# The last band of both 3x3 convolutions in mixed form, inside an attention-and-convolution kernel on one Trainium2 core

## The chip, the cores and the metric

The kernel runs on one core of a Trainium2 chip. The metric is the device time of one execution in microseconds (us); of several executions the median is taken. The engines are named as in the profile: PE is TensorE (PEld its weight loads), DVE is VectorE, ACT is ScalarE, POOL is GpSimd, SP is SyncE, which here only issues DMAs.

## The reference, cut to what matters

The input `x` is (4, 128, 64, 64) in float32: four images, 128 channels, 64 x 64 positions. Layer 0 is a group norm, a 4-head attention over the 4096 positions of each image, a projection and a residual. Layer 1, where the change lies, is a block of two 3x3 convolutions with weights quantized to 3 bits; its own input is the residual:

```python
residual = x
out = conv3x3_decomposed(x, lsq_quantize(w1, alpha1))
out = jax.nn.relu(batchnorm(out, gamma1, beta1))
out = conv3x3_decomposed(out, lsq_quantize(w2, alpha2))
out = batchnorm(out, gamma2, beta2)
out = jax.nn.relu(out + residual)
```

`batchnorm` takes the mean and the variance of each channel over all four images, so nothing behind a convolution can start before its last output is counted.

## The kernel before, in words

**Two parts.** Some nine tenths of the time go to the attention, in which the change touches nothing. Behind it come the two convolutions, one call each of `layer(i, prepare)`, with i = 0 and 1, and then a last pass that scales, adds the residual, applies relu and writes the output. All instructions stand in the order in which the code issues them; each engine runs its own in that order.

**Bands.** A convolution goes through 16 bands, four for each image. A band is 16 output rows, 1024 outputs for each channel, two PSUM banks of 512. `bandlist` holds them, and band m is its m-th entry, counted from 0; the last is band 15. Both operands of the convolution are float32 split in a high and a low part, so each product is done twice.

**Plain form.** `conv` (L830) computes 512 outputs with 18 matmuls of 512 columns, nine taps for the high and nine for the low part: 36 for a band. Its input is prepared by one cast on ACT (L619) and one subtraction on DVE (L622). It lies in rows of 66 columns with an empty column at each side (`raw_band`, L562), so in convolution 0 its load lands in runs of 64 elements; that of a band in mixed form has no side columns and lands in one run for each channel.

**Mixed form.** Two neighbouring output rows share work: from sums and differences of input rows and of weights (`mix_weights`) four products are formed, each three taps by two parts, six matmuls of 512 columns: 24 for a band (`conv_by_two`, L863). Two of them are the inner products a[0] and a[1], of which the even rows need the sum and the odd rows the difference; c[0] and c[1] are the outer products, one for the even and one for the odd rows. The price lies on the other engines. The input is prepared by `mixed_parts`: three subtractions and sums on DVE (`vo` L600, `vi` L602 and L603), two casts on ACT (`uo` and `ui`, L605), two more subtractions on DVE (`lo` and `li`, L609) and four small memsets on POOL (L596). The output is put together by `rows_of_two`: ACT copies a[1] (L886), DVE forms both inner results into the output `cv` (L889, L891), and the outer products are added either by a copy on ACT (L896 for one tile of two banks, L902 for two tiles of one) and an accumulating DMA that POOL issues (L904), or at once on DVE (L908). `BY_TWO` names the bands in mixed form: 2 to 14 before, of both convolutions.

**PSUM.** `banks(m)` hands out the banks of a mixed band. The inner products get a tile of two banks of the pool `pss` (three such tiles); the outer products get, in turn, either another `pss` tile (the names end in z) or two one-bank tiles of the pool `psa` (x and y; the pool has two).

**Order within a band.** The PE work of band m comes first, then `prepare(m)` gives the input preparation of band m + 2 (`begin`, `rest`) and the fetch of band m + 3 (`later`): in convolution 0 a load by SP (L628), in convolution 1 a relu on ACT that reads `cv` (L1147). On DVE the order is: the first three steps for band m + 2, the inner results of band m, the two last steps for band m + 2, and, where they are added at once, the outer results of band m. In convolution 0, bands 13 and 14 are added at once, and so in convolution 1 (`m > 12`).

**Statistics.** Plain bands go through `bn_stats` on DVE. For mixed bands the sums come with the instructions that form the outputs, and the sum of squares from a pass of ACT over the band (L1020), which can only run once the accumulating DMA has landed. These passes stand in the list `behind`, and `flush(1)` issues all but the newest.

**The end of a convolution.** `flush()` issues the squares that are left; DVE folds statistics into `end` (L1036 to L1044); the last band is done in plain form, half after half, with `bn_stats` (L1050) and a copy by ACT (L1051) for each; PE does ten small matmuls to stay busy (`keep_warm`, L315); `batch_norm` forms scale and shift (L926 to L935). In convolution 0 the next one then starts with relu on ACT (L1159).

**Residual loads.** The last pass needs the attention's output again (`load_res`, L1184). SP issues eight of these loads (512 KB each) as soon as the load of band 15 in convolution 0 is out, and eight more late in convolution 1, when the buffers of the pools `upper` and `kpool` come free.

Of the kernel before, what the change touches and what calls it, by code (L numbers as in the profile page):

```python
# [16 lines left out]
F32 = mybir.dt.float32  # L17
AF = mybir.ActivationFunctionType
ALU = mybir.AluOpType
# [3 lines left out]
P = 128  # L23
# [55 lines left out]
def _fast_body(ctx, tc, x, norm_w, norm_b, qkv_wt, qkv_b, proj_wt, proj_b,  # L79
# [152 lines left out]
    def f32(t):  # L232
        return t.bitcast(F32)
# [347 lines left out]

    BY_TWO = (set(range(2, 15)),) * 2

    def mixed_parts(t, name):

# [275 lines left out]
    def conv_by_two(parts, a, c, i):  # L863

        for m, ps, w in ((1, a[0], wmix[:, 0, :, :]), (2, a[1], wmix[:, 1, :, :]),
                         (0, c[0], wq[i][:, 0:3, :]), (3, c[1], wmix[:, 2, :, :])):
            n = 0
            for part in parts:
                for kw in range(3):
                    nc.tensor.matmul(ps.rearrange("p (r w) -> p r w", w=W), w[:, kw, :],  # L870
                                     part[m][:, :, kw : kw + W], start=(n == 0), stop=(n == 5))
                    n += 1

    def rows_of_two(a, c, both, y, sums, name, at_once):

        def of(t, e):
            return t.rearrange("p (r e w) -> p r e w", e=2, w=W)[:, :, e, :]

        even, odd = of(y, 0), of(y, 1)
        a0, a1, c0, c1 = (u.rearrange("p (r w) -> p r w", w=W) for u in (*a, *c))  # L880
        outer_rows = f32(stack_tile(f"co{name}"))[:, : 2 * FB]

        copied = outer_rows[:, :FB].rearrange("p (r w) -> p r w", w=W)

        def copy():
            nc.scalar.copy(copied, a1)  # L886

        def inner():
            nc.vector.scalar_tensor_tensor(even, copied, 1.0, a0, ALU.mult, ALU.add,  # L889
                                           accum_out=sums[:, 0:1])  # L890
            nc.vector.scalar_tensor_tensor(odd, copied, -1.0, a0, ALU.mult, ALU.add,  # L891
                                           accum_out=sums[:, 1:2])

        def outer():
            if both is not None:
                nc.scalar.activation(  # L896
                    outer_rows.rearrange("p (r e w) -> p e r w", e=2, w=W),
                    both.rearrange("p e (r w) -> p e r w", w=W), AF.Identity,
                    accum_out=sums[:, 2:3])
            else:  # L900
                for e, u in enumerate((c0, c1)):
                    nc.scalar.activation(of(outer_rows, e), u, AF.Identity,  # L902
                                         accum_out=sums[:, 2 + e : 3 + e])
            nc.gpsimd.dma_start(out=y, in_=outer_rows, accum_op=ALU.add)  # L904

        def outer_at_once():
            for e, u, v in ((0, even, c0), (1, odd, c1)):
                nc.vector.scalar_tensor_tensor(u, u, 1.0, v, ALU.mult, ALU.add,  # L908
                                               accum_out=sums[:, e : e + 1])

        return copy, inner, outer_at_once if at_once else outer, outer_rows
# [26 lines left out]
    def layer(i, prepare, start=None):  # L938
# [6 lines left out]
        sums = mid.tile([P, 4 * len(two)], F32, name=f"sums{i}")  # L945
        squares = mid.tile([P, len(two)], F32, name=f"squares{i}")
        shift = mid.tile([P, 2], F32, name=f"shift{i}")
        end = mid.tile([P, 18], F32, name=f"end{i}")
        n_plain, n_two = (float(len(u) * 2 * FB) for u in (plain, two))
        nc.gpsimd.memset(end[:, 0:1], n_plain)  # L950
        nc.gpsimd.memset(sums, 0.0)
# [4 lines left out]
        def flush(left=0):  # L956
            while len(behind) > left:
                behind.pop(0)()
# [26 lines left out]
        def banks(m):  # L985
            b, g = bandlist[m]
            a = conv_tile(i, b, g)
            if (len(two) - 1 - two.index(m)) % 2:
                c = [psa.tile([P, FB], F32, name=f"c{i}_{b}_{g}{j}", tag="a") for j in "xy"]
                both = None  # L990
            else:
                both = pss.tile([P, 2, FB], F32, name=f"c{i}_{b}_{g}z", tag="s")
                c = [both[:, j, :] for j in range(2)]
            return [a[:, j, :] for j in range(2)], c, both

        done = start(banks, stats, keep, origin) if start else {}
        for m, (b, g) in enumerate(bandlist[:-1]):
            if m in done and m not in BY_TWO[i]:
                continue
            begin, rest, later = prepare(m)  # L1000
            if m in BY_TWO[i]:
                if m in done:
                    a, c, both = done[m]
                else:
                    a, c, both = banks(m)
                    conv_by_two(ready[i, b, g], a, c, i)
                y = cv[b][:, 2 * g * FB : (2 * g + 2) * FB]
                k = two.index(m)
                copy, inner, outer, junk = rows_of_two(a, c, both, y, sums[:, 4 * k : 4 * k + 4], f"{i}_{m}",
                                                       m > 12)  # L1010
                copy()
                if i == 0 and m < 13:
                    flush(1)
                begin()
                flush(1)
                inner()
                rest()
                later()
                outer()
                behind.append(lambda y=y, k=k, junk=junk: nc.scalar.activation(  # L1020
                    junk, y, AF.Square, bias=shift[:, 1:2], accum_out=squares[:, k : k + 1]))
                continue
            ps = conv_tile(i, b, g)
            for j in range(2):
                conv(ready[i, b, g], ps[:, j, :], j, wq[i])
            begin()
            flush(1)
            rest()
            later()
            for j in range(2):  # L1030
                stats(m, j, ps)
                keep(m, j, ps)
            if m == 0:
                origin()
        flush()
        nc.vector.bn_aggr(end[:, 1:3], st.rearrange("p j s -> p (j s)"))  # L1036
        nc.vector.tensor_scalar(end[:, 2:3], end[:, 2:3], n_plain, None, ALU.mult)
        nc.vector.tensor_reduce(end[:, 4:5], sums, AX.X, ALU.add)
        nc.vector.tensor_reduce(end[:, 5:6], squares, AX.X, ALU.add)
        nc.vector.tensor_scalar(end[:, 4:5], end[:, 4:5], 1.0 / n_two, None, ALU.mult)  # L1040
        off = small.tile([P, 1], F32, name=f"off{i}", tag="rs")
        nc.vector.tensor_tensor(off, end[:, 4:5], shift[:, 0:1], ALU.subtract)
        nc.vector.tensor_tensor(off, off, off, ALU.mult)
        nc.vector.scalar_tensor_tensor(end[:, 5:6], off, -n_two, end[:, 5:6], ALU.mult, ALU.add)  # L1044
        b, g = bandlist[-1]
        for j in range(2):
            ps = psa.tile([P, FB], F32, name=f"c{i}_last{j}", tag="a")
            conv(ready[i, b, g], ps, j, wq[i])
            c = 2 * g + j
            nc.vector.bn_stats(end[:, 6 + 6 * j : 12 + 6 * j], ps)  # L1050
            nc.scalar.copy(cv[b][:, c * FB : (c + 1) * FB], ps)  # L1051
        for f in prepare(len(bandlist) - 1):
            f()
        if i == 0:
# [18 lines left out]
    def first(m):  # L1073
# [9 lines left out]
                mix()  # L1083

        def later():
            if m == 4:
                last["project"]()
                last["store"]()
                att.close()
                pools["low"] = ctx.enter_context(tc.tile_pool(name="low", bufs=1, reuse_waits="tile"))  # L1090
                cv.extend(pools["low"].tile([P, N], F32, name=f"cv{b}") for b in (2, 3))
            if m == 5:
                nc.sync.dma_start(out=f32(wq[1]), in_=wqd)
            if m == 11:
                scales()
            if m == 14:
                count_bad()
            if 2 < m < len(bandlist) - 3:
                load_band(*bandlist[m + 3])
# [572 lines left out]
```

## Time and profile before

| what | value |
|---|---|
| median of 4 executions | 2465.27 us (2464.58 to 2468.8) |
| the profiled execution | 2465.17 us |
| its span, first to last instruction | 2463.5 us |
| granted TensorE clock, mean | 0.995 |
| PE busy | 2430.5 us (99%) |
| DVE busy | 2199.1 us (89%) |
| ACT busy | 2183.3 us (89%) |
| convolution 0, its first matmul | 2224.9 us from the span's start |
| convolution 0, its last band on PE | from 2319.06 us |
| convolution 1, its first matmul | 2331.47 us |
| convolution 1, its last band on PE | from 2423.81 us |
| first instruction of the last pass | 2435.02 us |

All times inside the trace count from the first instruction of the span; 1.67 us of the profiled execution lie around it. In a timeline a row gives the start, the length, the engine, the line, the operation with output and input, how many instructions are merged in it, and in brackets how long the engine was idle before it and what ended that idle time. Starts of neighbouring instructions of an engine can lie closer together than their lengths.

### The profile page before, as it was taken

What the parts mean: (1) busy time and instruction counts of PE and PEld (TensorE: products, weight loads), DVE (VectorE), ACT (ScalarE), POOL (GpSimd) and SP (SyncE); (2) the same over time, 40 slices, a digit from 0 to 9 for tenths busy, and PEclk for the clock granted to TensorE, in tenths of its full rate; (3) what the DMA queues carried; (4) which work ended last, traced back from release to release, by engine and by line L of the source; (5) the groups of instructions that cost most, each with busy time, mean ns of one, the idle gap of its engine ahead of it and who ended that gap; (6) DMA issues with size and microseconds to landing.
All of it is one profiled execution on the core that took longest, in us unless ns stands there. A gap on an engine that the chain in (4) does not pass through costs nothing.

```text
span 2463.5 us, 65084 instructions
## 1 busy us (share of the span) xinstructions
PE 2430.5 (99%) x28384; PEld 1443.8 (59%) x28384; DVE 2199.1 (89%) x1566; ACT 2183.3 (89%) x2428; POOL 301.2 (12%) x530
## 2 busy tenths in 40 slices
PE   9999999999999999999999999999999999999995
PEld 6555555555555555555555555555555555557774
DVE  6899888989998888889989888898999999999797
ACT  6999888999988899999998899999999999996687
POOL 1111111111101111111101111111110100101110
PEclk9999999999999999999999999999999999999997
DMA  6877677778776766678767676678656666666637
GB/s 202 192 187 168 168 177 177 168 188 211 170 162 167 181 159 165 144 204 206 171 149 178 177 172 156 155 190 209 150 138 151 140 140 151 153 148 171 169 61 240
DMA packets 128533, 416.74 MB, mean 169 GB/s; under 512 B 33824, under 2 KB 34976, under 8 KB 99568
## 3 DMA queue, kind: packets, MB, share of 16 engines
q0 software_dynamic: 48832, 292.91, 52.6%
q1 hardware_dynamic: 78736, 118.28, 16.8%
q8 instruction: 225, 3.69, 0.6%
q10 hardware_dynamic: 672, 1.31, 0.1%
q14 instruction: 68, 0.56, 0.1%
HBM read 107.75 MB, written 56.43 MB: 67 GB/s over the span
## 4 chain that ended last, share of the span: by engine, by line
PE 98%; DVE 1%; issue 0%; DMA 0%; POOL 0%; ACT 0%; ACTq 0%; POOLq 0%; DVEq 0%
PE s L447 44%; PE acc L461 40%; PE c L870 3%; PE c L837 1%; PE po L322 1%; PE l L493 1%; PE pq L322 1%; PE pv L322 1%; PE pk L322 1%; PE c_2z L870 1%; PE c_0z L870 1%; PE c_last L837 1%; DVE res L1210 1%; PE idle L315 1%; PE c_1x L870 0%; PE c_3x L870 0%
## 5 line engine op out<-in xcount | busy, mean ns | idle before, releaser
L449 ACT ACTIVATE p<-s 128x1024 f32<-128x1024 f32 x2048 | 1951.3, 1033 | 194.9 <-PE s L447 150.4
L476 DVE TENSOR_TENSOR r<-r,p 128x2048 f32<-128x2048 f32 x768 | 1758.1, 2289 | 63.0 <-ACT p L449 11.9
L447 PE MATMUL s<-q,k 64*128 64x512 f32 x8192 | 1136.8, 409 | 0.6 <-DMA q<-qst 0.6
L461 PE MATMUL acc<-p,v 128*32 128x256 f32 x16384 | 1025.8, 383 | 0.0
L447 PEld LDWEIGHTS s<-q,k 64*128 64x128 f32 x8192 | 715.6, 184 | 407.2 <-issue 164.8
L461 PEld LDWEIGHTS acc<-p,v 128*32 128x32 f32 x16384 | 462.7, 109 | 483.2 <-issue 248.1
L471 POOL DMA_DIRECT2D rm<-p x160 | 140.4, 877 | 782.3 <-ACT p L449 632.4
L357 DVE SCALAR_TENSOR_TENSOR kst<-pk,b,kst 128x512 fp32r<-128x512 f32 x32 | 24.0, 750 | 81.2 <-PE s L447 61.4
L474 DVE TENSOR_TENSOR r<-p,p 128x2048 f32<-128x2048 f32 x32 | 73.2, 2287 | 8.6 <-ACT p L449 8.6
L357 DVE SCALAR_TENSOR_TENSOR qst<-pq,b,qst 128x512 fp32r<-128x512 f32 x32 | 24.0, 751 | 59.0 <-PE s L447 48.0
L361 POOL DMA_DIRECT2D qd<-qst x31 | 23.0, 742 | 269.3 <-DVE qst L357 220.0
L497 POOL DMA_DIRECT2D r<-rm x32 | 27.2, 851 | 223.6 <-PE s L447 97.1
L870 PE MATMUL c<-li,wmix 128*128 128x512 f32 x156 | 45.8, 401 | 0.0
L870 PE MATMUL c<-ui,wmix 128*128 128x512 f32 x156 | 45.8, 401 | 0.0
L361 POOL DMA_DIRECT2D kd<-kst x27 | 20.0, 741 | 174.3 <-DVE kst L357 159.0
L469 POOL DMA_DIRECT2D rm<-p x32 | 17.8, 557 | 173.7 <-ACT p L449 99.8
L1020 ACT ACTIVATE co<-cv,shift 128x1024 f32<-128x1024 f32 x26 | 29.9, 1149 | 10.2 <-DMA cv<-co 10.2
L493 PE MATMUL l<-r,ones 128*32 128x256 f32 x512 | 37.7, 379 | 0.0
L605 ACT CAST uo<-vo 128x1024 fp32r<-128x1024 f32 x26 | 27.3, 1050 | 10.9 <-DVE vo L600 9.9
L538 POOL DMA_DIRECT2D y<-x x32 | 21.2, 661 | 120.6 <-DVE x L537 120.6
L356 ACT ACTIVATE kst<-pk,b 128x512 fp32r<-128x512 f32 x32 | 22.3, 700 | 15.2 <-PE pk L322 13.0
L904 POOL DMA_DIRECT2D cv<-co x22 | 19.0, 864 | 126.9 <-ACT co L902 41.7
(224 smaller groups left out, 1231.8 us busy)
## 6 DMA issues: line engine op xcount, KB each, us to landing
rm<-p POOLq DMA_DIRECT2D x192, 1024.0 KB, 7.8
r<-rm POOLq DMA_DIRECT2D x32, 1024.0 KB, 7.6
q<-qd SPq DMA_DIRECT2D x248, 128.0 KB, 4.4
x<-in_x_dram SPq DMA_DIRECT2D x86, 256.0 KB, 6.1
k<-kd SPq DMA_DIRECT2D x124, 128.0 KB, 4.7
qd<-qst POOLq DMA_DIRECT2D x31, 512.0 KB, 5.0
kd<-kst POOLq DMA_DIRECT2D x27, 512.0 KB, 4.4
cv<-co POOLq DMA_DIRECT2D x22, 512.0 KB, 4.7
```

Source lines behind the costliest of these rows:

```text
L322: nc.tensor.matmul(out[cs, :], w[:, cs], x, start=True, stop=True)
L357: nc.vector.scalar_tensor_tensor(lo, ps[what], bias, t[:, 0, :], ALU.add, ALU.subtract)
L361: (nc.sync if start else nc.gpsimd).dma_start(out=dst[b, j].rearrange("s p n -> p s n"), in_=t)
L447: nc.tensor.matmul(s[:, i, :], k[r, half, c0 : c0 + P], q[r, half, part, :], start=(part == 0), stop=(part == 1))
L449: nc.scalar.activation(pts[step][:, 2 * half : 2 * half + 2, :], s, AF.Exp, scale=SCALE)
L461: nc.tensor.matmul(acc[n][h * D : (h + 1) * D, cs], v[:, kt % KB, h * D : (h + 1) * D], pt[:, h, cs], start=(kt == 0 and half == 0), stop= ...
L471: nc.gpsimd.dma_start(out=msum[n], in_=pt, accum_op=ALU.add)
L474: nc.vector.tensor_tensor(rsum[n], pts[step - 1], pt, ALU.add)
L476: nc.vector.tensor_tensor(rsum[n], rsum[n], pt, ALU.add)
L493: nc.tensor.matmul(t["l"][h * D : (h + 1) * D, cs], ones, r[:, h, cs], start=first, stop=end)
L837: nc.tensor.matmul(ps.rearrange("p (r w) -> p r w", w=W), w[:, tap, :], part[:, r0 + kh : r0 + kh + RB, kw : kw + W], start=(n == 0), stop ...
L870: nc.tensor.matmul(ps.rearrange("p (r w) -> p r w", w=W), w[:, kw, :], part[m][:, :, kw : kw + W], start=(n == 0), stop=(n == 5))
```

## The change

Band 15 of both convolutions goes over to the mixed form. Its matmuls are written out anew (`last_by_two`): the inner products first, a[1] ahead of a[0], then c[0], then c[1] in two halves of four rows, that is in matmuls of 256 columns. Its output is put together on DVE alone: the inner sum and difference, the outer product for the even rows and its `bn_stats`, then for each half of the odd rows the outer product and its `bn_stats`. `end` grows by one group of six for the third `bn_stats`.

Some things move with it. Fewer of the folding steps stand ahead of the last band's work, and the two that need the squares now stand between the two halves. Band 14 no longer calls `flush(1)`, so three square passes are issued at the end, behind the copy of a[1] of band 15. In convolution 0, band 13 is no longer added at once but by the accumulating DMA (`m > 13 - i`). The turn of z and x/y is reversed for all mixed bands, since it is now counted back from band 15. The projection and the store of the last attention block come one band earlier (m == 3).

```diff
-    BY_TWO = (set(range(2, 15)),) * 2
+    BY_TWO = (set(range(2, 16)),) * 2
...
+    def last_by_two(parts, a0, a1, c0, c1, i):
+
+        half = RB // 2
+        halves = [c1[:, j * half * W : (j + 1) * half * W] for j in range(2)]
+        for m, rows, ps, w in ((2, slice(0, RB), a1, wmix[:, 1, :, :]),
+                               (1, slice(0, RB), a0, wmix[:, 0, :, :]),
+                               (0, slice(0, RB), c0, wq[i][:, 0:3, :]),
+                               (3, slice(0, half), halves[0], wmix[:, 2, :, :]),
+                               (3, slice(half, RB), halves[1], wmix[:, 2, :, :])):
+            n = 0
+            for part in parts:
+                for kw in range(3):
+                    nc.tensor.matmul(ps.rearrange("p (r w) -> p r w", w=W), w[:, kw, :],
+                                     part[m][:, rows, kw : kw + W], start=(n == 0), stop=(n == 5))
+                    n += 1
...
-        end = mid.tile([P, 18], F32, name=f"end{i}")
+        end = mid.tile([P, 24], F32, name=f"end{i}")
...
-            if (len(two) - 1 - two.index(m)) % 2:
+            if (len(bandlist) - 1 - m) % 2:
...
-                                                       m > 12)
+                                                       m > 13 - i)
                 copy()
                 if i == 0 and m < 13:
                     flush(1)
                 begin()
-                flush(1)
+                if m < 14:
+                    flush(1)
...
-        flush()
+        b, g = bandlist[-1]
+        (a0, a1), (c0, c1), _ = banks(len(bandlist) - 1)
+        last_by_two(ready[i, b, g], a0, a1, c0, c1, i)
         nc.vector.bn_aggr(end[:, 1:3], st.rearrange("p j s -> p (j s)"))
         nc.vector.tensor_scalar(end[:, 2:3], end[:, 2:3], n_plain, None, ALU.mult)
         nc.vector.tensor_reduce(end[:, 4:5], sums, AX.X, ALU.add)
-        nc.vector.tensor_reduce(end[:, 5:6], squares, AX.X, ALU.add)
         nc.vector.tensor_scalar(end[:, 4:5], end[:, 4:5], 1.0 / n_two, None, ALU.mult)
         off = small.tile([P, 1], F32, name=f"off{i}", tag="rs")
         nc.vector.tensor_tensor(off, end[:, 4:5], shift[:, 0:1], ALU.subtract)
         nc.vector.tensor_tensor(off, off, off, ALU.mult)
-        nc.vector.scalar_tensor_tensor(end[:, 5:6], off, -n_two, end[:, 5:6], ALU.mult, ALU.add)
-        b, g = bandlist[-1]
+        copied = f32(stack_tile(f"ca{i}"))[:, :FB]
+        nc.scalar.copy(copied, a1)
+        flush()
+        y = cv[b][:, 2 * g * FB : (2 * g + 2) * FB].rearrange("p (r e w) -> p e r w", e=2, w=W)
+        even, odd = y[:, 0], y[:, 1]
+        a0, c0, c1, copied = (u.rearrange("p (r w) -> p r w", w=W) for u in (a0, c0, c1, copied))
+        nc.vector.tensor_tensor(even, copied, a0, ALU.add)
+        nc.vector.tensor_tensor(odd, a0, copied, ALU.subtract)
+        nc.vector.tensor_tensor(even, even, c0, ALU.add)
+        nc.vector.bn_stats(end[:, 6:12], even)
+        half = RB // 2
         for j in range(2):
-            ps = psa.tile([P, FB], F32, name=f"c{i}_last{j}", tag="a")
-            conv(ready[i, b, g], ps, j, wq[i])
-            c = 2 * g + j
-            nc.vector.bn_stats(end[:, 6 + 6 * j : 12 + 6 * j], ps)
-            nc.scalar.copy(cv[b][:, c * FB : (c + 1) * FB], ps)
+            if j == 1:
+                nc.vector.tensor_reduce(end[:, 5:6], squares, AX.X, ALU.add)
+                nc.vector.scalar_tensor_tensor(end[:, 5:6], off, -n_two, end[:, 5:6], ALU.mult, ALU.add)
+            rows = odd[:, j * half : (j + 1) * half, :]
+            nc.vector.tensor_tensor(rows, rows, c1[:, j * half : (j + 1) * half, :], ALU.add)
+            nc.vector.bn_stats(end[:, 12 + 6 * j : 18 + 6 * j], rows)
...
-            if m == 4:
+            if m == 3:
                 last["project"]()
```

## The prediction

> **What bounds it now.** I read the timelines of PE, DVE and ACT around the two ends, then the waits, then the DMA views. All times are of the profiled execution (2465.17 us, 0.10 under the median of the runs shown, so a difference carries over).
>
> End of convolution 0, PE and then DVE:
>
> ```profile
> 2319.06 2.31 PE L837 MATMUL c_last<-hi,wq 128*128 128x512 f32 x9
> 2321.20 2.31 PE L837 MATMUL c_last<-lo,wq 128*128 128x512 f32 x9
> 2323.36 2.30 PE L837 MATMUL c_last<-hi,wq 128*128 128x512 f32 x9
> 2325.49 2.31 PE L837 MATMUL c_last<-lo,wq 128*128 128x512 f32 x9
> ...
> 2329.22 2.50 PE L315 MATMUL idle<-gavg 128*128 128x128 f32 x20 [1.29 <-ACT cv L1051]
> 2331.47 2.39 PE L837 MATMUL c<-hi,wq 128*128 128x512 f32 x9
> ```
> ```profile
> 2324.30 0.17 DVE L1039 TENSOR_REDUCE end<-squares 128x1 f32<-128x14 f32 x1 [3.31 <-ACT co L1020]
> ...
> 2327.84 0.70 DVE L1050 BATCH_NORM_STATS2 end<-c_last 128x6 f32<-128x512 f32 x1 [2.12 <-PE c_last L837]
> 2328.58 0.24 DVE L926 BATCH_NORM_AGGREGATE bmv<-end 128x2 f32<-128x18 f32 x1
> ```
>
> PE ends last: DVE waits 2.12 us for it, then does one `bn_stats`, and the final aggregate starts at 2328.58. That start is my mark for convolution 0; all that follows hangs on it. Nine matmuls of 512 columns start 2.145 us apart, 0.2385 each; 36 are 8.6 us.
>
> End of convolution 1, DVE and then PE:
>
> ```profile
> 2417.37 1.22 DVE L609 TENSOR_TENSOR li<-vi,ui 128x1024 fp32r<-128x1024 f32 x1
> 2420.07 0.69 DVE L889 SCALAR_TENSOR_TENSOR cv<-co,c 128x512 f32<-128x512 f32 x1 [1.49 <-ACT co L886]
> ...
> 2429.67 0.17 DVE L1039 TENSOR_REDUCE end<-squares 128x1 f32<-128x13 f32 x1 [2.86 <-ACT co L1020]
> ...
> 2432.60 0.70 DVE L1050 BATCH_NORM_STATS2 end<-c_last 128x6 f32<-128x512 f32 x1 [1.51 <-PE c_last L837]
> 2433.33 0.23 DVE L926 BATCH_NORM_AGGREGATE bmv<-end 128x2 f32<-128x18 f32 x1
> ```
> ```profile
> 2417.83 0.89 PE L870 MATMUL c<-ui,wmix 128*128 128x512 f32 x3
> 2418.73 0.95 PE L870 MATMUL c<-li,wmix 128*128 128x512 f32 x3
> ```
>
> Here the bands before the last no longer go at PE's pace. The `li` matmuls start 0.90 after the `ui` ones instead of 0.72, just behind the end of `li` on DVE at 2418.59; bands 12 to 14 follow each other in 5.98 us, where 24 matmuls are 5.72. DVE has no idle time from 2353 to 2418.6. Only the plain last band gives it 1.49 + 2.86 + 1.51 = 5.86 us of rest. Mark: 2433.33.
>
> **PE.** Band 15 drops from 36 matmuls to 18 of 512 columns and 12 of 256. The latter are not in the trace: half of 0.2385 (0.119) at best, 0.2385 at worst. The `idle` matmuls of 128 columns start 0.117 apart; the line between 128 and 512 columns gives 0.157, which I take. 18 x 0.2385 + 12 x 0.157 = 6.18 us instead of 8.59: PE gains 2.41 each time (2.9 to 1.4).
>
> The matmuls' 128-column weight loads take 188 ns here and matmuls of 400 ns start every 239 ns, so loads overlap. [...]
>
> **DVE, what comes in.** For each convolution:
> - Input of band 15: vo 1.14, vi twice 0.60, lo and li 1.14 each, start to start, is 4.6 us; the plain subtraction (1.31) goes.
> - Output: even and odd sums at 0.60 each, the even outer sum 0.60 and then 0.71 to its end, since `bn_stats` needs it, then `bn_stats` 0.62. The halves have no row. Rows of 1024 and 512 elements (1.218, 0.683) give 0.535 for each 512 and a fixed 0.148, so 0.42 for a sum of 256 and 0.43 for its `bn_stats` (bounds: half and all of 0.69). The two `bn_stats` of 512 go.
> - The folding steps stay, about 1.04 us, most of them now straight in front of this.
>
> **Convolution 0.** DVE has room in the middle: the 1.71 us before band 14's inner sums, the 3.31 above, and band 13's outer sums (1.22), which leave it for ACT, POOL and DMA. `li` of band 15 ends at 2317.8, over 1 us before PE needs it. Then, from the copy of a[1] of band 14 on ACT (2318.0, behind two casts, one square pass and the outer copy of band 13): inner sums of band 14 to 2319.3, bad count to 2319.6, its outer sums to 2320.8, folding to 2321.9. a[0] of band 15 is complete at 2319.06 + 2.9 = 2322.0, c[0] at 2323.5, the halves of c[1] at 2324.4 and 2325.4. Even and odd sums to 2323.2; even outer sum 2323.55 to 2324.25; `bn_stats` and first half to 2325.75; squares and their step 0.3; second half 2325.98 to 2326.85. Aggregate at 2326.88: **1.70 us earlier**, of PE's 2.41; DVE is late next.
>
> Hidden only while two things hold. ACT's square passes of bands 13 and 14 (1.13 each) must be over by 2325.6, so band 13's accumulating DMA must land by about 2323.2. It is issued at 2317.5, so 5.7 us are left; behind that wait stand the pass of band 14 on ACT, then DVE's squares, second half and the aggregate. And ACT must empty band 13's outer banks before PE starts c[0] of band 15 (2321.9; I have 2317.6).
>
> ```profile
> DMA to landing us min/median/max: 4.4/4.7/10.8
> ```
> ```profile
> DMA packets 3779, 6.36 MB, mean 212 GB/s; under 512 B 2368, under 2 KB 2368, under 8 KB 3776
> ```
>
> The first is the group of accumulating DMAs, the second the traffic from 2300 to 2330. The long landings (10.8 and 9.4) are those of bands 11 and 12, beside SP's eight residual loads; the traffic ends at 2322.4. The change also thins it: band 15's load (17 x 128 = 2176 pieces of 256 bytes) becomes 128 pieces. The hardware queue's share there (48.5% of 30 us x 16 engines = 233), less 1024 pieces of 4 KB at 0.146 (from the same queue beside convolution 1), leaves 36 ns a small piece; the saving is some 63 of engine time, 3.9 us on 16 engines. Old traffic then ends near 2318.5 and I take 4.6 for the landing: 2322.1, about 1 us to spare. If the thinning is worth nothing, 2322.4 + 2.7 = 2325.1.
>
> **Between the convolutions.** `keep_warm` no longer waits for the last ACT copy and runs by 2327.7, so PE idles about 2 us ahead of convolution 1 instead of 1.29. The clock allows it:
>
> ```profile
> 2437.00:2438.00 1.00, 0.00 (x0) 0.00 (x0) 1.00 (x2) 0.53 (x2) 0.00 (x0) 1.00 0.61 227
> 2438.00:2439.00 1.00, 0.00 (x0) 0.00 (x0) 1.00 (x2) 0.95 (x2) 0.00 (x0) 0.66 0.81 297
> ```
>
> The column behind POOL's count is the granted clock: it falls at about 2438.3, 3.5 us after the last matmul ended (2434.8). If it fell in the 2 us gap, PE would run at half speed for a few us; DVE reads band 0's last sums at 2345.4, 5 us after PE has them, so up to 3 us of it cost little.
>
> **Convolution 1** starts 1.70 earlier and then runs at the same pace, since it is DVE and ACT that set it. Reversing z and x/y moves 0.14 us on ACT (1.00 against 1.14) from one band to the next and back. In the times of before, DVE goes on without rest from 2418.66: vo, vi, vi to 2421.0, inner sums of band 13 to 2422.2 (filling the 1.49), lo and li to 2424.5, outer sums of 13, inner and outer of 14 to 2428.1, folding to 2429.2, then the list above: 2430.4, 2431.1, 2431.7, 2432.5, squares 2432.8, second half 2433.65. PE is done by 2430.2, and ACT's squares, even with band 12's DMA landing at 2427.6 instead of 2426.1 (residual loads move nearer to it, waiting for band 13's buffers instead of band 12's), by 2431.1. The aggregate starts at 2433.68, **0.35 later** than 2433.33. PE's whole gain is lost there.
>
> POOL gains eight memsets of 0.4 us and one issue (0.85) and idles over 13 us at both ends: nothing. SP's two last residual loads now wait for band 12's square pass (2428.7) and are needed by the last pass after 2449: nothing. The projection moved forward finds its operand ready at 2251.3 and starts at 2254.8: nothing; bounds of these three together, -0.2 to +0.3.
>
> **Sum:** -1.70 + 0.35 = -1.35, so 2465.17 - 1.35 = **2463.8 us**. The half costs on both sides give -2.4 to -0.3.
>
> **Rivals.**
> 1. *PE's gain comes through at both ends*, because DVE's steps are shorter or better hidden: each mark then follows PE by one half sum and one `bn_stats` (0.95 instead of 0.83), 2.3 each: 2460.6. Against: convolution 1 has only 5.86 us of DVE rest for 3.3 + 2.8 new. Only in convolution 0: 2463.2.
> 2. *The accumulating DMA of band 13 lands late.* The price starts at 2323.2 and counts in full. Landing at 2325.1: +1.9, 2465.7. With the worst row, 10.8 us: 2328.3, +5.1, 2468.9, **slower than before**. For: both landings beside it took over 9. Against: the old traffic is nearly gone.
> 3. *The clock falls in the gap*, or the reversed banks hold PE up in the middle of a convolution: up to 1.7 for the clock, more for a stall in each band: 2465 to 2471. Against: the 3.5 us above, and every bank has been empty over 1 us before its next use.
> 4. *No change*: both ends DVE-bound as convolution 1 is: 2465.2.
>
> **Chances.** Forecast with its range (2462.8 to 2464.9) 0.55; rival 1 0.15, mostly its weaker half; rival 2 0.18; rival 3 0.05; rival 4 0.07. The range 2461.2 to 2466.8 leaves out the full rival 1 and the worst of 2 and 3. A difference of 0.2% is 4.9 us, about what a measurement of this kernel can tell from no change: faster by more 0.03, within 0.92, slower by more 0.05.
>
> **What would show it.** Right: PE's last band near 6.2 us; in convolution 0 the second-half sum on DVE follows its own queue and not ACT; aggregate 1.7 earlier; in convolution 1 DVE idle nowhere behind `li` of band 14, the two aggregates 105.1 us apart instead of 104.75. Wrong: DVE's squares (L1075 after the change) waiting over 0.5 us for ACT, PE idle inside a band, or a granted clock under 1 at the start of convolution 1.

## The result, and the profile after

The changed kernel takes 2468.04 us in the median of 40 executions (2466.51 to 2472.8), beside 2465.33 for the kernel before on the same chip (60 executions, 2464.11 to 2468.8): ratio 1.001, 95% interval 1.0006 to 1.0015. It is 2.7 us slower, where a kernel 1.35 us faster (2463.8 us) was forecast, and lies outside the range given. The profiled execution took 2467.58 us, its span 2465.9 us, mean clock 0.993.

Two marks make the kernels comparable, since the time ahead of them differs from run to run: band 15 of convolution 0 begins between 2318.11 and 2321.20 us in the profiles below. **D0** is the time from the first matmul of band 15 of convolution 0 to the final aggregate of that convolution; **D1** is from there to the aggregate of convolution 1. Before, D0 is 2328.58 - 2319.06 = 9.52 and D1 104.75. After, D0 is 2329.05 - 2318.69 = 10.36 and D1 106.87. Forecast were 9.52 - 1.70 = 7.82 and 105.10.

The end of convolution 0 in the changed kernel, timeline of PE (each of the ten small matmuls has two rows, hence x20):

```profile
2318.69 0.88 PE L886 MATMUL c<-ui,wmix 128*128 128x512 f32 x3
...
2322.26 0.88 PE L886 MATMUL c_3z<-lo,wq 128*128 128x512 f32 x3
...
2324.06 0.53 PE L886 MATMUL c_3z<-lo,wmix 128*128 128x256 f32 x3
...
2324.64 2.50 PE L315 MATMUL idle<-gavg 128*128 128x128 f32 x20
2331.79 4.18 PE L837 MATMUL c<-hi,wq 128*128 128x512 f32 x9 [4.66 <-POOL li L596]
```

PE does what was hoped for, and more: band 15 is over at 2324.6 instead of 2327.8. But then it stands still for 4.66 us, and the first nine matmuls of convolution 1 take 4.18 us instead of 2.39.

ACT and then DVE in the same stretch:

```profile
2321.73 0.59 ACT L1063 COPY ca<-c 128x512 f32<-128x512 f32 x1 [3.96 <-PE c L886]
...
2325.46 1.15 ACT L1037 ACTIVATE co<-cv,shift 128x1024 f32<-128x1024 f32 x1 [2.00 <-DMA cv<-co]
```
```profile
2322.35 0.69 DVE L1068 TENSOR_TENSOR cv<-ca,c 128x512 f32<-128x512 f32 x1 [0.75 <-ACT ca L1063]
...
2324.62 0.69 DVE L1070 TENSOR_TENSOR cv<-cv,c_3z 128x512 f32<-128x512 f32 x1 [0.98 <-PE c_3z L886]
...
2327.86 0.17 DVE L1075 TENSOR_REDUCE end<-squares 128x1 f32<-128x14 f32 x1 [1.04 <-ACT co L1037]
...
2329.05 0.26 DVE L942 BATCH_NORM_AGGREGATE bmv<-end 128x2 f32<-128x24 f32 x1
```

Three waits are new. The copy of a[1] starts at 2321.73, though a[1] was complete at 2320.3; the even outer sum starts at 2324.62, though c[0] was complete at 2323.14 (2322.26 + 0.88): each begins when the *last* matmul into its two-bank tile is done, a[0]'s for the copy (2321.70), and that of the second half of c[1] for the sum (2324.59). And the square pass of band 13 waits 2.00 us for band 13's accumulating DMA; band 14's pass and DVE's `squares` stand behind it.

The granted clock (the column behind POOL's count) shows what the standstill did:

```profile
2329.00:2330.00 1.00, 0.00 (x0) 0.00 (x0) 0.50 (x3) 0.00 (x0) 0.35 (x1) 0.94 0.00 0
2330.00:2331.00 1.00, 0.00 (x0) 0.00 (x0) 0.51 (x4) 0.18 (x1) 1.00 (x16) 0.50 0.00 0
...
2336.00:2337.00 1.00, 1.00 (x4) 0.76 (x4) 0.60 (x1) 1.00 (x2) 0.00 (x0) 0.65 0.00 0
```

A mean of 0.94 over a microsecond that begins at 1.00 and ends at 0.50 puts the fall at 2329.88; 0.65 puts the return at 2336.70. Between them convolution 1 ran at half speed for 4.9 us. Before, the clock stood at 1.00 through this whole stretch.

The end of convolution 1, ACT and then DVE:

```profile
2431.19 1.15 ACT L1037 ACTIVATE co<-cv,shift 128x1024 f32<-128x1024 f32 x1 [1.92 <-DMA cv<-co]
```
```profile
2431.58 0.69 DVE L1070 TENSOR_TENSOR cv<-cv,c_3z 128x512 f32<-128x512 f32 x1 [0.51 <-PE c_3z L886]
...
2434.73 0.17 DVE L1075 TENSOR_REDUCE end<-squares 128x1 f32<-128x13 f32 x1 [0.95 <-ACT co L1037]
...
2435.92 0.27 DVE L942 BATCH_NORM_AGGREGATE bmv<-end 128x2 f32<-128x24 f32 x1
```

Again DVE waits for squares behind a late DMA. The landing times of the last accumulating DMA of convolution 0 and of convolution 1, issued at 2317.6 and 2420.6, and the traffic of 2300 to 2330:

```profile
DMA to landing us min/median/max: 7.8/7.8/7.8
```
```profile
DMA to landing us min/median/max: 10.5/10.5/10.5
```
```profile
DMA packets 1875, 6.88 MB, mean 229 GB/s; under 512 B 208, under 2 KB 208, under 8 KB 1872
...
q1 hardware_dynamic: 1296, 4.75, 44.9%
```

The 2000-odd small pieces are gone, but the hardware queue's share fell only from 48.5% to 44.9% of 480 engine-us (16 DMA engines for 30 us). This queue carries SP's loads, `software_dynamic` (q0) the accumulating DMAs that POOL issues: in e8, which keeps the residual loads back, it moves 0.56 MB from 2300 to 2330 instead of 4.75, and q0 2.10 as here. The trace shows microsecond by microsecond which of them moves (a share counts the time that packets took; here it reaches 106.6%). From 2320 to 2321 the hardware queue has 101.1% and q0 0.1%; from 2322 to 2323 it is 3.0% and 102.4%. So band 13's DMA, issued at 2317.6, moves next to nothing until the residual loads are through (band 12's, ahead of it in q0, landed at 2320.6). In convolution 1 nothing is ahead of band 12's DMA in q0, band 11's having landed at 2419.4, and yet from 2421 to 2426 the hardware queue has 82 to 107% in each microsecond and q0 at most 2%; the DMA issued at 2420.6 moves from 2426 on.

### The profile page after: what moved, and what is told of

Same layout as the page of the kernel before. It is cut to its first block, busy times and chain, and to the rows that moved or that the text cites. A ratio compares the mean times of both kernels' runs of the same rounds, so it can differ in the third digit from the quotient of the medians.

```text
span 2465.9 us, 65106 instructions
## 1 busy us (share of the span) xinstructions
PE 2425.4 (98%) x28372; PEld 1440.6 (58%) x28372; DVE 2210.3 (90%) x1582; ACT 2185.4 (89%) x2434; POOL 302.6 (12%) x535
## 4 chain that ended last, share of the span: by engine, by line
PE 93%; DVE 3%; DMA 1%; issue 1%; ACT 1%; POOL 0%; ACTq 0%; SPq 0%; POOLq 0%; DVEq 0%
PE s L447 44%; PE acc L461 39%; PE c L837 2%; PE c L870 1%; PE l L493 1%; PE pq L322 1%; PE po L322 1%; PE pk L322 1%; PE pv L322 1%; DMA cv<-co 1%; DVE res L1238 1%; DMA res<-y 0%; PE c_3z L870 0%; DVE li L609 0%; DVE vo L600 0%
## 5 line engine op out<-in xcount | busy, mean ns | idle before, releaser
L609 DVE TENSOR_TENSOR lo<-vo,uo 128x1024 fp32r<-128x1024 f32 x28 | 34.1, 1219 | 2.0 <-ACT uo L605 2.0
L356 ACT ACTIVATE kst<-pk,b 128x512 fp32r<-128x512 f32 x32 | 22.3, 699 | 15.2 <-PE pk L322 13.1
L600 DVE TENSOR_TENSOR vo<-t 128x1024 f32<-128x1024 f32 x28 | 34.1, 1219 | 1.7 <-DMA t<-y 1.0
```

## Experiments

The theory after the result: **three things** took the gain and more: late landings of the accumulating DMAs in front of the squares (both convolutions), waits on whole tiles (convolution 0), and the clock between the convolutions. Rivals: the clock alone; DVE's own load alone. The third part of the theory fell for the changed kernel, but for one way that stays open, as shown below. The times of e1 to e15 are medians of 10 or 11 executions (e4: one), beside the kernel before on the same chip (2465.17 to 2465.40 in the four series). Their intervals reach about 0.1%, 2.4 us, to either side, so most of these medians alone can't be told apart; the marks and the rows carry the argument.

| kernel | us | D0 | D1 |
|---|---|---|---|
| before | 2465.33 | 9.52 | 104.75 |
| after | 2468.04 | 10.36 | 106.87 |
| e1 convolution 0 alone | 2468.12 | 11.08 | 106.28 |
| e2 convolution 1 alone | 2466.55 | - | 105.59 |
| e3 whole, 22 small matmuls | 2467.87 | 10.00 | 105.80 |
| e4 as e2, no late loads (one run) | 2464.39 | - | 105.13 |
| e5 whole, own tiles | 2467.27 | 11.27 | 105.89 |
| e6 convolution 0, band 13 at once | 2465.61 | 9.22 | 104.83 |
| e7 as e6, own tiles | 2463.80 | 7.77 | 104.87 |
| e8 convolution 0, loads later | 2465.43 | 9.22 | 104.84 |
| e9 e7 again | 2463.59 | 8.13 | 104.88 |
| e10 e9 and convolution 1 | 2464.94 | 8.27 | 105.57 |
| e11 e9 without halves | 2463.68 | 7.95 | 104.85 |
| e12 e9 without small matmuls | 2465.09 | 8.25 | 106.54 |
| e13 convolution 0, 22 small matmuls | 2466.61 | 11.91 | 106.62 |
| e14 e10 without late loads | 2464.58 | 8.19 | 105.23 |
| e15 whole, both landings freed, 22 small matmuls | 2465.27 | 9.21 | 105.20 |

The marks are of one profiled execution each, the times are medians; the profiled ones of e3, e6 and e7 were the fastest of their ten (2465.98, 2464.5, 2462.73), those of e1 and e13 the slowest of theirs (2470.6 and 2470.52).

**Which convolution (e1, e2).** `LAST` names the convolutions that have the changed tail; the others keep the old one, its width of `end` and its turn of z and x/y. In e2 and e4 the projection of the last attention block also stays where it was (m == 4).

```diff
-    BY_TWO = (set(range(2, 16)),) * 2
+    LAST, WARM = {0}, (10, 10)
+    BY_TWO = tuple(set(range(2, 16 if i in LAST else 15)) for i in range(2))
...
```

> The change in convolution 0 alone; convolution 1 ends in plain form as before. Two distances tell the theories apart: D0, from the first matmul of band 15 of convolution 0 to its final aggregate (9.52 us before, 10.36 after the change), and D1, from there to the aggregate of convolution 1 (104.75 before, 106.87 after). Every theory expects D0 near 10.4. Clock theory (PE idles too long ahead of convolution 1, runs at half speed and never makes it up): PE reaches its last band 1.4 us late and, since the plain last band is bound by PE, D1 is 106.1, total 2467.5. If the loss of convolution 1 comes only from the late accumulating DMA or from DVE's added work there, D1 is 104.8 and the total 2466.2.

> The change in convolution 1 alone; convolution 0 and the small matmuls behind it are as before, so the clock should stay at 1.00 between the two. D0 9.5. Landing theory (band 12's accumulating DMA lands late beside the residual loads, and the square passes queue behind it): the landing takes about 10.5 us again, DVE waits for the squares, D1 106.7, total 2467.3. Clock theory: without the slow stretch D1 is 105.1 to 105.4, total 2465.8. The recorded forecast (DVE's own work): D1 105.1, DVE without a wait behind li of band 14.

e1: 2468.12 us, ratio 1.0009 (1.0000 to 1.0019); the clock fell, D1 is 106.28 where its theory said 106.1, and D0 is 0.7 longer than every theory had it. e2: 2466.55, ratio 1.0006 (0.9996 to 1.0016); D1 105.59 lies between the theories. Each alone is slower in the median, though the second interval includes 1, and the two do not add up (2.8 + 1.2 against 2.7); why is seen under the clock.

**The clock (e3, e12, e13).** `keep_warm(22)` behind convolution 0 (e3: whole change; e13: convolution 0 alone), and none at all in the best kernel (e12).

```diff
-        keep_warm(10)
+        keep_warm(WARM[i])        # e3, e6, e8, e13, e15: (22, 10); e12: (0, 10)
```

> The whole change, with 22 small matmuls instead of 10 behind convolution 0, 2.8 us more of them, so that PE idles some 2 us instead of 4.7. The clock should stay at 1.00. D0 stays near 10.4. Clock theory: D1 falls from 106.9 to 105.4, total 2466.4. Landing theory: PE comes 1.4 us earlier to its last band and nothing is won, since the square passes wait for the same DMA: D1 106.5 to 106.9, total 2467.7.

> Change in convolution 0 alone with 22 small matmuls behind it, all else of its tail as changed (band 13 by the accumulating DMA beside the residual loads, two-bank tiles). Theory that the late landing is the larger cost in convolution 0: 2466.4 to 2467.2, against 2465.4 to 2465.6 with band 13 at once or the loads later; D0 10.2 to 11.2, D1 104.8. Theory that the clock was nearly all of it: 2465.3 to 2465.8 and D0 at 9.5.

> As e9, but without the 10 small matmuls behind convolution 0, so that PE stands still some 4 us from its last matmul of band 15 to the first of convolution 1. It prices the clock by itself. Theory of the clock: it falls to 0.5 some 2 to 4 us after the last matmul and comes back 4 to 7 us later, D1 105.4 to 106.4 instead of 104.87, time 2464.4 to 2465.3. If the clock costs nothing there (convolution 1 hides it): D1 104.8 to 105.0 and the time as e9.

e12 prices the clock by itself: 2465.09 against 2463.59 in e9, 1.5 us, and D1 106.54 against 104.88. Its windows show the fall at 2329.56 and the return at 2336.38. PE stood still before the first matmul of convolution 1:

```profile
2330.49 4.18 PE L838 MATMUL c<-hi,wq 128*128 128x512 f32 x9 [4.04 <-POOL li L597]
```

But in e9 and e12 convolution 1 has its old tail, and PE sets its end. In e3, the whole change with the clock held, the median is near that of the change (2467.87, ratio 1.001, 1.0001 to 1.002). Its profiled run has D1 1.07 shorter, between the two theories, which looked like the clock; D1 split at the issue of band 12's accumulating DMA shows where the difference lies. From the aggregate of convolution 0 to that issue:

| kernel | clock | to the issue | issue to square pass | D1 |
|---|---|---|---|---|
| after | fell | 91.54 | 10.60 | 106.87 |
| e5 | fell | 91.53 | 9.63 | 105.89 |
| e3 | held | 91.55 | 9.52 | 105.80 |
| e2 | held | 91.46 | 9.41 | 105.59 |
| e10 | held | 91.56 | 9.28 | 105.57 |
| e15 | held | 91.54 | 7.62 | 105.20 |

In e15 the pass waits for no DMA, in the others it does. The time to the issue is the same with and without the fall: DVE and ACT pace convolution 1, and up to there they lose nothing. PE does (its band 15 begins 96.59 us after the aggregate in the changed kernel, 95.40 in e3, and DVE waits 0.51 for c[0]), but behind that DVE waits for the squares anyway. So up to that issue **the clock costs nothing that shows**, and the whole difference in D1 to e3 lies in the landing behind it (10.60 against 9.52).

One way in which the clock can still reach D1 leads through that landing. The first late residual load starts when PE's last `ui` matmuls of band 13 are done (2416.50 and 2416.58 in the changed kernel, 2414.53 and 2414.60 in e3), and PE is behind where the clock fell: counted from the aggregate of convolution 0, the load starts at 87.53 in the changed kernel and 86.78 in e5, but at 85.93 to 86.03 in e2, e3 and e10. The landing took 10.5 us in the first, 9.5 in e5 and 9.2 to 9.4 in the other three. So later loads may be why it took longest in the changed kernel; no run moves them alone, and e5 shows little of it.

In e1, where PE sets the end of convolution 1, the fall costs some 1.4 us of D1 (106.28 against 104.83 to 104.88 with the old tail and the clock held), near the 1.66 of e12. That can account for the sum: without 1.5 us for the clock, e1 and e2 add up to 2.5 of the 2.7.

e13's median (2466.61, ratio 1.0007, 0.9997 to 1.0016) is what the theory of the landing named. Its profiled run missed D0 (11.91, where 11.2 was the most) and D1: the squares came so late that 22 small matmuls ended 3.5 us before convolution 1 began, and the clock fell again.

**The late landings (e4, e6, e8, e14, e15).** e6: band 13 of convolution 0 is added on DVE. e8 and e15: each residual load of images 0 and 1 waits for a small write into its tile. e4, e14 and e15: those of images 2 and 3 become a memset.

```diff
-                                                       m > 13 - i)
+                                                       m > (12, 12)[i])   # e6
...
+        if b in (2, 3):                      # e4, e14, e15
+            nc.gpsimd.memset(t, 0.0)
+            return
+        if b < B - 2:                        # e8, e15
+            nc.gpsimd.memset(t[:, 0:1], 0.0)
         nc.sync.dma_start(out=t, in_=y0[b][:, i * HN : (i + 1) * HN])
```

> As the run with convolution 1 alone, but the eight residual loads of images 2 and 3 are left out (POOL writes zeros in their place, so the residual of these two images is missing from the output). Landing theory: band 12's accumulating DMA lands in about 4.7 us instead of 10.5, DVE no longer waits for the squares, D1 105.1 to 105.4. If the waits come from elsewhere, D1 stays at 106.7.

> Change in convolution 0 alone (convolution 1 keeps the old tail), 22 small matmuls behind it, and band 13's sums made at once on DVE, without its accumulating DMA, so that the squares of bands 13 and 14 wait for no DMA. Theory of the late landing: DVE's wait for the squares (1.04 us in the changed kernel) goes, D0 falls from 10.36 to about 9.3, limited then by the tile-wide waits; D1 104.8 since the clock holds; time 2464.9 to 2465.3. Theory of tile-wide waits alone: D0 10.1 to 10.4 and time 2465.8 to 2466.1. If DVE's two more sums of band 13 are what costs, D0 rises above 10.4.

> Change in convolution 0 alone with 22 small matmuls, band 13 by the accumulating DMA as in the changed kernel, but the loads of the residual of images 0 and 1 are kept back by a small POOL write into their tile, so that most of them run later. Theory of contention: band 13's accumulating DMA lands 4.4 to 5 us after its issue, not 7.8, the squares wait less, D0 9.3 to 9.5 and the time 2465.0 to 2465.5. Theory that the DMA is long by itself or held by its queue's earlier ones: the landing stays at 7 us or more and D0 at 10.3. If the loads kept back collide with later work instead, D1 rises above 104.8.

> As e10 (convolution 0 with band 13 at once and own tiles, convolution 1 with the changed tail and own tiles), but the residual loads of images 2 and 3 are left out, and with them the residual of those images, so that nothing stands beside band 12's accumulating DMA. Theory that the late landing makes e10's loss and spread: D1 105.1 to 105.3, time 2463.7 to 2464.2 and ten runs within 1.5 us. Rival that DVE's load in convolution 1 makes them: median 2464.6 to 2465.2, ten runs over 2.5 us or more as in e10 (2463.3 to 2466.6). Leaving out the loads may itself save something at the very end, so the marks count for more than the time.

> The whole change, both tails as changed, with 22 small matmuls behind convolution 0, the residual loads of images 0 and 1 kept back by a small POOL write, and those of images 2 and 3 left out with their residual. If landings and clock are the whole loss, the tile-wide waits remain: D0 9.2 to 9.4, D1 105.1 to 105.3, time 2465.4 to 2465.9, against 2468.0 of the change. If something else costs, it stays at 2466.5 or above.

In convolution 0 the two ways to free the squares agree: D0 9.22 with band 13 at once and 9.22 with the loads later, where the DMA landed in 4.6 us instead of 7.8 (8.0 in e13, the same kernel with its loads in place); times 2465.61 (ratio 1.0001, 0.9992 to 1.0011) and 2465.43 (0.9998, 0.9988 to 1.0008). The start of band 13's square pass, counted from the first matmul of band 15, gives D0 wherever that pass waits for the DMA:

| kernel | square pass of band 13 | D0 | difference |
|---|---|---|---|
| e3 | 6.41 | 10.00 | 3.59 |
| after | 6.77 | 10.36 | 3.59 |
| e1 | 7.48 | 11.08 | 3.60 |
| e5 | 7.68 | 11.27 | 3.59 |
| e13 | 8.32 | 11.91 | 3.59 |

In convolution 1 the aggregate starts 4.72 or 4.73 us behind the start of band 12's square pass wherever it waits for the DMA (the changed kernel, e2, e3, e5 and e10). With no late loads that DMA lands in 4.5 us (e14, e15) instead of 9.2 to 10.5, no pass waits, and D1 is 105.13 to 105.23.

e15 closes the account: with both landings free (and the clock held), the whole change takes 2465.27 us (ratio 1.0001, 0.9991 to 1.001). Loads left out may help the last pass too (from the second aggregate to the end of the span it is 29.7 us in e15, 30.0 in the changed kernel and 30.2 before), so the marks count for more: D0 + D1 is 117.23 in the changed kernel, 114.41 in e15 and 114.27 before. All but 0.14 of the loss is gone. Its DVE rows have no wait at the squares; two waits are left, both for whole tiles, 1.37 us for the copy of a[1] and this one:

```profile
2324.61 0.69 DVE L1080 TENSOR_TENSOR cv<-cv,c_3z 128x512 f32<-128x512 f32 x1 [0.98 <-PE c_3z L887]
...
2326.72 0.15 DVE L1085 TENSOR_REDUCE end<-squares 128x1 f32<-128x14 f32 x1
...
2327.89 0.26 DVE L943 BATCH_NORM_AGGREGATE bmv<-end 128x2 f32<-128x24 f32 x1
```

e14 is not clear: its marks are the theory's, but its median (2464.58; ratio 0.9997, 0.9987 to 1.0007) lies at the edge of the rival's, and its spread of 1.8 us between the two.

**The tiles (e5, e7, e9).** e5: the whole change, each product of band 15 in a tile of its own. e7 and e9: this together with e6, ten small matmuls.

```diff
-        (a0, a1), (c0, c1), _ = banks(len(bandlist) - 1)
+        a1, a0, c0 = (pss.tile([P, 2, FB], F32, name=f"c{i}_{b}_{g}{n}", tag="s")[:, 0, :] for n in "pqr")
+        c1 = [psa.tile([P, FB], F32, name=f"c{i}_{b}_{g}{n}", tag="a")[:, : FB // 2] for n in "st"]
...
```

> The whole change, but every product of the last band in a PSUM tile of its own (a[1], a[0], c[0], and the two halves of c[1]), so that a copy or sum waits for its own matmuls alone. Marks: D0 is from the first matmul of band 15 of convolution 0 to its aggregate (10.36 us in the changed kernel), D1 from there to the aggregate of convolution 1 (106.87). Theory of tile-wide waits: they set the end of convolution 0; the copy of a[1] starts 1.4 us earlier, the sum of c[0] 1.0 earlier, D0 falls to 8.9 to 9.4, and the time to about 2466.4. Theory of the late landing (squares of bands 13 and 14 behind band 13's accumulating DMA): the copy and sums start earlier but DVE then waits longer for the squares, D0 stays within 0.3 of 10.36 and the time at 2467.5 to 2468. In both, the small matmuls now wait for the second half sum, start some 2 us later and cover more of the gap, so that the clock holds and D1 is 105.4 to 106.0 if the clock was the second cost, and 106.9 if not.

> As the kernel with band 13 at once in convolution 0 alone, and with each product of the last band in a tile of its own (10 small matmuls, which now wait for the second half sum). Both theories together: last matmul at 5.9 us from the start of band 15, half a sum 0.4, half statistics 0.4, two small sums hidden or 0.3, aggregate 0.3 and three gaps of 0.1 to 0.2, D0 7.9 to 8.4; D1 104.8; time 2464.0 to 2464.4, 1 us below the kernel before. If a third thing (DVE's own load in bands 13 to 15) sets the end, D0 stays at 9.3 or above and the time at 2465 or above.

> The kernel with the changed tail in convolution 0 alone, band 13 at once and own tiles, again in more rounds for a narrower interval. Theory (PE's gain of about 1.7 us in convolution 0 comes through once the late DMA and the tile-wide waits are gone): time 2463.5 to 2464.0, 0.9994 of the kernel before, D0 7.8 and D1 104.8 again. If the earlier ten runs were a chance: 2465.0 to 2465.5.

In e5 the copy of a[1] did start 1.62 us behind the first matmul instead of 3.04, and it brought nothing: DVE, earlier at the squares, waited 3.10 us there instead of 1.04 (ratio 1.0007, 0.9998 to 1.0017). Two points of the expectation failed: D0 rose to 11.27, because the DMA landed 0.9 later, counted from band 15's first matmul (issued 0.4 later and 8.3 us under way instead of 7.8), and the clock fell, since the small matmuls now waited for a sum behind those squares:

```profile
2329.20 4.63 PE L315 MATMUL idle<-gavg 128*128 128x128 f32 x20 [4.07 <-DVE cv L1089]
```

With the squares free, own tiles do count: D0 9.22 becomes 7.77 (e7) and 8.13 (e9, the same kernel; 8.19 to 8.27 in e10, e12 and e14, which have this tail too), the time 2465.61 becomes 2463.80 and 2463.59. That is most or all of the gain that was forecast for convolution 0 (7.82). DVE has no wait left in e9:

```profile
2323.88 0.68 DVE L1100 TENSOR_TENSOR cv<-cv,c_3r 128x512 f32<-128x512 f32 x1
...
2325.98 0.15 DVE L1105 TENSOR_REDUCE end<-squares 128x1 f32<-128x14 f32 x1
...
2327.15 0.26 DVE L943 BATCH_NORM_AGGREGATE bmv<-end 128x2 f32<-128x24 f32 x1
```

This is the best version found: ratio 0.9994 (0.9985 to 1.0004) and, in the second series, 0.9993 (0.9984 to 1.0002). Both series are 1.6 to 1.8 us below the kernel before; each interval just reaches 1.

**Convolution 1 and the halves (e10, e11).** e10 is e9 with `LAST = {0, 1}`. e11 is e9 with c[1] as one product of 512 columns, one sum and one `bn_stats`:

```diff
-                               (3, slice(0, half), halves[0], wmix[:, 2, :, :]),
-                               (3, slice(half, RB), halves[1], wmix[:, 2, :, :])):
+                               (3, slice(0, RB), c1, wmix[:, 2, :, :])):
...
```

> As e9, and convolution 1 with the changed tail and own tiles as well (band 12 there still by its accumulating DMA). Theory (DVE sets the end of convolution 1, and the late landing adds): D0 7.8 as in e9, D1 105.1 to 105.9, time 2464.2 to 2464.9, above e9. Rival (with own tiles PE's gain comes through in convolution 1 too): D1 102.7 to 103.5, time 2461.7 to 2462.5.

> As e9 without the halves: the last outer product in one tile of 512 columns, one sum and one statistics. Theory that the last matmul sets the end, so that halves pay: the whole sum and statistics (0.69 each) come behind it instead of half ones (0.41 and 0.43), D0 8.1 to 8.3 instead of 7.8, time 2464.1 to 2464.4. Rival that DVE sets the end already there: two halves take DVE 0.4 to 0.5 us longer than one whole, D0 7.4 to 7.6, time 2463.4 to 2463.6.

e10: 2464.94 us (ratio 0.9999, 0.9989 to 1.0008), 1.35 above e9; D1 105.57 with own tiles too, so PE's gain does not come through there. e11: 2463.68 (0.9993, 0.9984 to 1.0002), D0 7.95, between the two theories and between e7 and e9: the halves bring nothing that can be seen. DVE works without rest in e9 and e11, so that no sum waits for the last matmul there, and the odd rows' sums and `bn_stats` take it 0.78 and 0.91 us as halves (e9), 1.44 as a whole (e11), from start to start.

Other expectations were missed by little: the times of e6, e7 and e15 by 0.1 to 0.3 us, that of e1 by 0.6, and the marks of e7, e8, e9, e10 and e12 by 0.1 to 0.5.

## Why the prediction was wrong, step by step

- **PE, right and better.** Halves start 0.121 apart (three in 0.36) where 0.157 was taken; PE gains 8.59 - (18 x 0.238 + 12 x 0.121) = 2.85, at the good end of the bounds.
- **DVE's half sum and half statistics, right:** 0.40 to 0.42 and 0.43, as taken.
- **Convolution 0, failed at two steps.** First, "I take 4.6 for the landing: 2322.1": it took 7.8, and the pass behind it began at 2325.46, 6.77 us behind the first matmul of band 15. The price was to start at 2323.2, 4.14 behind it; the 2.6 us between are about the 2.54 by which D0 missed. The term that was mis-sized is the thinning of band 15's load: 3.9 us were taken off the traffic, 63 engine-us at 36 ns a small piece (its own figures give 60), so that the old traffic would end near 2318.5. It ended near 2322: the queue's time fell by at most (48.5 - 44.9)% of 480 = 17 engine-us, 1.1 us on 16 engines. The text's own case "if the thinning is worth nothing, 2325.1" is what came, 7.6 us under way, and that is rival 2; the issue also came 0.5 us later against band 15 than was taken. It sets D0 (the table of differences). Second, the list of completion times assumed that each sum waits for its own product. With two products in a tile it waited for both: 0.9 to 1.4 us of D0 (9.22 against 7.77 to 8.27). It was hidden behind the landing in the changed kernel.
- **Between the convolutions, failed, at no direct cost.** The gap was put at 2 us; with the aggregate late it became 4.66, and a fall 3.5 us after the last matmul was read from one row; here it came after 2.7. But "up to 3 us of it cost little" held with the changed tail, up to the issue of band 12's DMA (91.54 with the fall, 91.46 to 91.56 without); where PE sets the end of convolution 1 the fall costs 1.66 (e12), the size of rival 3.
- **Convolution 1, DVE's part right:** 0.35 was forecast, e4, e14 and e15 give 105.13 to 105.23, that is 0.4 to 0.5 over 104.75. **Its landing failed:** band 12's DMA was forecast to land at 2427.6 in the times of before, 99.0 us behind the aggregate of convolution 0; it landed 102.1 behind it (2431.1), and DVE waited 0.95 for the squares. The step said that the residual loads move nearer and charged 1.5 us for it. SP issued the first of them at 2408.50 before and at 2416.58 after, 7.6 us later against that aggregate, and all eight within 8.5 us instead of 15.2; beside them the DMA took 10.5 us instead of 6.2.
- **The sum:** 7.82 became 10.36 (+2.54) and 105.10 became 106.87 (+1.77), together 4.31 over the forecast of 2463.8: 2468.1, where the median is 2468.04. Rival 2 came true, and in both convolutions; the prediction had priced it in convolution 0 alone, so that its middle case read 2465.7 and its range ended at 2466.8.

**Open:** how much convolution 1 costs in the median. Marks say 0.4 without late loads; the medians say 1.0 (e14 against e9) and -0.2 (e15 against e8). Why band 12's DMA took 1 us longer in the changed kernel's profile than in e2, e3, e5 and e10 is open too, and with it whether the clock had a part in it; one profile each can't tell chance from cause.

## What to carry to other kernels

When PE stops being the last at a join, list every transfer that a pass in front of the join waits for and price its landing from rows beside the *same* traffic; a landing in a quiet stretch (4.5 us here) says little about one beside eight 512 KB loads (7.8 to 10.5). Consumers of one product should get a tile of their own where they end the chain (D0 9.22 became 7.77 to 8.27 here), but first free whatever they queue behind: alone, own tiles moved only a wait (e5). And a mechanism that is found at one end of a loop is to be priced at every end.

## What the runs showed of the hardware that was not expected

In five profiles the clock fell between the convolutions, and in four of them it stayed at 0.50 for the same time within 0.02 us. Each edge is worked out from the mean clock of its microsecond, as above for the changed kernel:

| kernel | mean at the fall, at the return | fall | return | time at 0.50 |
|---|---|---|---|---|
| after | 0.94, 0.65 | 2329.88 | 2336.70 | 6.82 |
| e1 | 0.77, 0.81 | 2333.54 | 2340.38 | 6.84 |
| e5 | 0.70, 0.89 | 2327.40 | 2334.22 | 6.82 |
| e12 | 0.78, 0.81 | 2329.56 | 2336.38 | 6.82 |
| e13 | 0.75, - | 2334.50 | after 2341.00 | over 6.50 |

In e13 the clock still reads 0.50 from 2340 to 2341, and nine matmuls take 2.32 us again from 2342.28. The time at 0.50 is the same whether matmuls resumed 1.5 us (e1) or 0.9 us (e12) behind the fall. The fall itself came 2.7 us after the last matmul's end in the changed kernel, 3.9 in e1, 2.3 in e5, 3.1 in e12, 2.8 in e13, and 3.5 at the end of the kernel before. Between the convolutions all five gaps in PE's work of 3.5 us or more (3.52 in e13 to 5.37 in e1) brought a fall, and none of 1.6 us or less did (the longest is 1.61, in e3). No profile has a gap of a length in between, and none shows why the delay differs from run to run.

The 2176 pieces of 256 bytes cost the DMA engines hardly more than their bytes in larger pieces. With the same 4.75 MB on the hardware queue from 2300 to 2330 its share reads 48.5% with the small pieces (before) and 44.9% without (the changed kernel), some 17 engine-us in all. With the same 5.34 MB from 2295 to 2332 it reads 44.3% before, 41.6% in the changed kernel and 42.4% in e3, that is 16 and 11 of 592 engine-us: 5 to 8 ns a piece.
